# A decoder layer on one core: seven products for eight over both halves of a down product, and work moved off VectorE

## The chip, the cores and the metric

The kernel runs on one core of a Trainium2 chip. The metric is the device time of one execution in microseconds (us). The engines are TensorE (PE, with PEld for its weight loads), VectorE (DVE), ScalarE (ACT), GpSimd (POOL) and SyncE (SP), each with a queue that it works through in order; DMA transfers are issued from the queues of SP and POOL.

## What is computed

One decoder layer over x of 2 x 512 tokens with 1024 features, all in fp32, with three normalisations:

```
x = layernorm(x + attention(x))        # per token: 32x32 scores between features d and e, over 32 heads
x = layernorm(x + crossing(x, ctx))    # fake_quant(x) @ fake_quant(ctx), 8 bits, ctx 1024x1024
x = layernorm(x + ffn(x))              # below
h = relu(x @ up) ** 2                  # up 1024x2048
latent = x @ fc1                       # fc1 1024x512
moe = (latent @ expert) * (sum of the two largest of x @ gate)
ffn = layernorm(h @ down + moe @ fc2, gamma, beta)     # down 2048x1024, fc2 512x1024
```

The attention mixes features within a token: scores are (d, e) for each token, summed over heads, with a softmax over e. It is therefore elementwise work and reductions on VectorE, not matmuls.

## The kernel before

The 1024 tokens are eight tiles of 128 (`NT = 8`), paired in four blocks of 256 tokens (`TB = 2` tiles a block). The product expert·fc2 is made once (`e2`), so that the end of the ffn is one product: the 2048 squares and 512 latents of a token, as `h` of five groups (`NG = 5`) of four slices of 128 (`piece`), times the rows of down and of e2.

In time the kernel goes: a front of 142.5 us (q, k, v of all tiles, e2, attention and crossing of tiles 0 and 1), then block 0 (`ffn`, its up and fc1 products at line 827 until 219 us, and its down product `down`, line 1057, until 296 us), then block 1 (up and fc1 until 376 us, its down product `down_halved` until 450.4 us), then blocks 2 and 3 together (`ffn_pair`, `down_pair`, from 454.7 us) until the end at 697.3 us. While TensorE multiplies for blocks 0 and 1, VectorE does the attention of tiles 2 to 7, whose results the pair needs.

Several generators make this order. `token_path` walks through the tiles: `scores` (lines 474 and 480, a multiplication of 128x2048 and a reduction, four of each a tile), `attend` (lines 507 and 513, the same number), `cross`. `ffn` walks through the matmuls of a block and is paced against the token path by weights (`w_ffn`, `w_tok`). Side work stands in the list `later`, and `beside(n)` steps each entry n times after a product; `tc.issue_after(x)` keeps an instruction behind x in the scheduler's order, and within that the scheduler of the framework sets the queues. `behind_products` keeps transposes and products in the order of the program on TensorE, behind the latest matmul.

`cross` quantises a tile into `a` (a pass on ACT of `below_top` for most tiles, `quantise` on VectorE for the two of the front, which are `hurried`), transposes it (`pta`, line 652) into `aT` by a copy on ACT (line 653), multiplies by the codes of the context (`py`, line 665), and adds that to `xc` (lines 658, 659 and 670). `between` holds the score steps of the next tile, placed in its middle. Then `normalise_aside` normalises with ACT and POOL: sums, squares (line 351), the power on POOL (line 355) and the scaled pass (line 360). The context's tiles are made into codes by `context_beside`, with three tiles loaded ahead.

PSUM has two banks for `product` (`ps_mm`), four for the down products (`ps_dn`) and two for transposes (`ps_tr`). In `ffn` a relu on ACT (line 843) empties a product bank, and a second pass (line 844) squares it into `h`. In `down` (block 0) the columns are done in halves of 512 with plain products of 128x512; at the end `finish` takes each tile straight from PSUM on VectorE: statistics (lines 324 and 326), a scaled difference with gamma (line 1006), and the sum with xc (line 1013, which also sums for the last normalisation), then `store_aside`.

`down_halved` (block 1) makes its left 512 columns with plain products (line 1109): for each group and slice k, one matmul for each of the two tiles. Its right 512 columns go by a scheme of seven products for eight (line 1129). The block is seen as 2 x 2: the two tiles by the two column quarters of 256, with the contraction in pairs of slices. VectorE makes sums of the weights (`sums_of`, lines 1097 to 1100, four of 128x512 a group) and of `h` (lines 1088 to 1091, four of 128x256), and TensorE does seven products of 128x256 for each of two slices:

```
1088  nc.vector.tensor_tensor(s1, a21[:, g], a22[:, g], ALU.subtract)
...
1097  nc.vector.tensor_tensor(t1, b11, b12, ALU.add)
```

The seven products collect over the five groups in four PSUM banks (1 and 6, 7 and 5, 4, 2 and 3), and after the last group VectorE combines them into `c11` to `c22`. The two tiles are then normalised with gamma in `ended_later`.

Of the kernel before, what the change touches and what calls it, by code (L numbers as in the profile page):

```python
# [16 lines left out]
P = 128  # L17
EPS = 1e-5
# [9 lines left out]
def kernel(  # L28
# [288 lines left out]

    def mean_rstd(halves, name, stats=None):
# [9 lines left out]
        nc.vector.tensor_scalar_add(ve, mv[:, 1:2], EPS)  # L328
# [4 lines left out]
    def normalise(t, name):  # L333

        mean, rstd = mean_rstd([t[:, ts(h, HALF)] for h in range(E // HALF)], name)
        return nc.vector.tensor_scalar(t, t, mean, rstd, ALU.subtract, ALU.mult)
# [25 lines left out]
    def quantise(dst, src, tmp, rs, z):  # L362

        nc.vector.tensor_scalar(tmp, src, rs, z, ALU.mult, ALU.add)
        nc.vector.tensor_scalar(tmp, tmp, 0.0, QMAX, ALU.max, ALU.min)
        nc.vector.tensor_scalar(dst, tmp, ROUND, ROUND + CENTRE, ALU.add, ALU.subtract)
# [100 lines left out]
    def scores(t, qk, behind=None):  # L467
# [3 lines left out]
        for c in range(D // DC):  # L471
            prod = tokp.tile([P, DC * D * G], F32, tag="prod", name=f"pqk_{t}_{c}", bufs=2)
            with tc.issue_after(behind.ins) if behind is not None else ExitStack():
                nc.vector.tensor_tensor(  # L474
# [5 lines left out]
            nc.vector.tensor_reduce(  # L480
                s[:, ts(c, DC), :].rearrange("p d e -> p (d e)"),
                prod.rearrange("p (c g) -> p c g", g=G), AX.X, ALU.add,
            )
            yield 4.6
# [12 lines left out]
    def attend(t, xc, s, v):  # L497
# [7 lines left out]
        for c in range(D // DC):  # L505
            prod = tokp.tile([P, DC * D * G], F32, tag="prod", name=f"pav_{t}_{c}", bufs=2)
            nc.vector.tensor_tensor(  # L507
                prod.rearrange("p (d g e) -> p d g e", d=DC, g=G),
                s[:, ts(c, DC), :].unsqueeze(2).to_broadcast([P, DC, G, D]),
                v.unsqueeze(1).to_broadcast([P, DC, G, D]),  # L510
                ALU.mult,
            )
# [9 lines left out]
        if t == TB - 1:  # L522

            nc.vector.tensor_tensor(x3, x3, o3, ALU.add)
            normalise(xc, f"1_{t}")
# [23 lines left out]
    def context_beside(b):  # L549


        stages = {}

        def load(k):
            if k < KC:
                stages[k] = pools["sums"].tile([P, E], F32, tag="tt", name=f"ctx_{b}_{k}")

                nc.gpsimd.dma_start(stages[k], ctx_in[b, ts(k, P), :])

        passes = {}  # L560
        for k in range(3):
            load(k)
        for k in range(3):
# [7 lines left out]
        for k in range(KC):  # L571
# [9 lines left out]
            load(k + 3)  # L581
# [34 lines left out]
    def cross(t, xc, cq, crow, between):  # L616
# [6 lines left out]
        if hurried:  # L623

            quantise(a, xc, tmp, rs1, z1)
# [14 lines left out]
        else:  # L640
# [7 lines left out]
            yield from between  # L648
# [6 lines left out]
        behind = ExitStack if hurried or t == NT - 1 else lambda: tc.issue_after(lowered[0].ins)  # L655
        r = small.tile([P, 1], F32, tag="r", name=f"r_{t}")
        with behind():
            nc.vector.tensor_mul(r, total, s12d2)
# [18 lines left out]
        else:  # L677
            yield 3.0
            last = yield from normalise_aside(xc, sums, f"2_{t}")
            yield 6.0  # L680
        return last

    def token_path():


        batch, last = None, None
        at, done = {}, {}

        def begin(t):
# [5 lines left out]
            at[t] = xc, v, scores(t, qk, last if t == TB else None)  # L695
# [13 lines left out]
        for blk in range(NBLK):  # L709
            xcs = []  # L710
            x2T = []
            for i in range(TB):
# [4 lines left out]
                if t == 0:  # L717

                    begin(1)
                    yield next(at[1][2])  # L720
                yield from attend(t, xc, done[t], v)
# [6 lines left out]
                last = yield from cross(t, xc, *batch, between)  # L728
# [86 lines left out]
    def ffn(blk, xcs, xT):  # L815
# [21 lines left out]
        for c in range(INT // CW):  # L837
# [9 lines left out]
            if c in (1, INT // CW - 2):  # L847
                next(routing)
        for c in range(LAT // CW):
            w = wstream.tile([P, KE, CW], F32, tag="wa", name=f"fc1_{blk}_{c}")  # L850
            nc.sync.dma_start(w, fc13[:, :, ts(c, CW)])
            for i in range(CW // P):
# [12 lines left out]
        yield from (down if blk < PAIR - 1 else down_halved)(blk, h)  # L865
# [180 lines left out]
    def down(blk, h):  # L1046
# [16 lines left out]
        for i in range(TB):  # L1063
            finish(blk, i, new_y(blk, i), pd[i])

    def down_halved(blk, h):

        def rows_of(g, n):
            count[0] += 1
            pool, tag = (pools["more"], "wc") if count[0] % 3 == 0 else (wstream, "wb")  # L1070
            w = pool.tile([P, 4, HALF], F32, tag=tag, name=f"dn_{blk}_{n}_{g}")
            src, at = (dn3, 4 * g) if 4 * g < NI else (e23, 4 * g - NI)
            rows_loaded[0] = nc.sync.dma_start(w, src[:, at : at + 4, ts(n, HALF)])
            return w
# [3 lines left out]
        )  # L1078
        units, weights = {}, {}

        def sums_of(g):
            w = rows_of(g, 1)
# [3 lines left out]
            ss = pools["more"].tile([P, 4, 2, P], F32, tag="ss", name=f"units_{blk}_{g}", bufs=3)  # L1086
            s1, s2, s3, s4 = (ss[:, q] for q in range(4))
            nc.vector.tensor_tensor(s1, a21[:, g], a22[:, g], ALU.subtract)
            nc.vector.tensor_tensor(s2, s1, a11[:, g], ALU.subtract)
            nc.vector.tensor_tensor(s3, a11[:, g], a21[:, g], ALU.subtract)  # L1090
            nc.vector.tensor_tensor(s4, a12[:, g], s2, ALU.add)
            units[g] = {
                1: a11[:, g], 2: a12[:, g], 3: s4, 4: a22[:, g], 5: s1, 6: s2, 7: s3
            }
            tt = pools["sums"].tile([P, 3, 2, QW], F32, tag="tt", name=f"halved_{g}")
# [5 lines left out]
            weights[g] = {1: b11, 2: b21, 3: b22, 4: t4, 5: t1, 6: b12, 7: t3}  # L1101

        pd = [ps_dn.tile([P, HALF], F32, tag="dn", name=f"pd_{blk}_{i}") for i in range(TB)]
        for g in range(NG):
            w = rows_of(g, 0)
            for k in range(4):
                for i in range(TB):
                    with behind_products():
# [462 lines left out]
```

## Time and profile before

| what | value |
|---|---|
| time, median of 3 runs | 699.71 us (699.28 to 700.66) |
| the profiled execution | 699.09 us, span 697.3 us |
| mean granted clock of TensorE in it | 0.993 |
| TensorE busy | 677.7 us, 97% |
| VectorE busy | 607.5 us, 87% |
| ScalarE busy | 263.7 us, 38% |
| GpSimd busy | 76.0 us, 11% |
| block 1, plain left half (line 1109) | 80 records of 128x512, 376.9 to 416.1 us with other work between |
| block 1, seven-product right half (line 1129) | 140 records of 128x256, 416.1 to 450.4 us |

A matmul in fp32 leaves two records, so 80 records are 40 matmuls. The times of the profile are from the start of the span. A line of a timeline names start, length, engine, source line, operation, what it writes and reads, and in brackets the idle time before it and what ended that. In the windows, a row gives start and end, the length, the busy time with the number of instructions of PE, PEld, DVE, ACT and POOL, the granted clock of TensorE as a share, the share of the DMA engines and GB/s. In the list of waits the three numbers are the total, how often, and the longest.

### The profile page before, as it was taken

What the parts mean: (1) busy time and instruction counts of PE and PEld (TensorE: products, weight loads), DVE (VectorE), ACT (ScalarE), POOL (GpSimd) and SP (SyncE); (2) the same over time, 40 slices, a digit from 0 to 9 for tenths busy, and PEclk for the clock granted to TensorE, in tenths of its full rate; (3) what the DMA queues carried; (4) which work ended last, traced back from release to release, by engine and by line L of the source; (5) the groups of instructions that cost most, each with busy time, mean ns of one, the idle gap of its engine ahead of it and who ended that gap; (6) DMA issues with size and microseconds to landing.
All of it is one profiled execution on the core that took longest, in us unless ns stands there. A gap on an engine that the chain in (4) does not pass through costs nothing.

```text
span 697.3 us, 7629 instructions
## 1 busy us (share of the span) xinstructions
PE 677.7 (97%) x2862; PEld 494.6 (71%) x2872; DVE 607.5 (87%) x724; ACT 263.7 (38%) x443; POOL 76.0 (11%) x107
## 2 busy tenths in 40 slices
PE   8999999999999999999999999999999999999991
PEld 4666654578877444478877458788888888888881
DVE  5899987699999999799999987698778679897895
ACT  1287543222635449627726215311144200000252
POOL 1012112200011122002001000020011000000012
PEclk9999999999999999999999999999999999999997
DMA  9999628394545548455535534695887545557733
GB/s 335 302 335 366 156 25 299 102 305 144 166 135 160 193 140 292 136 180 189 176 126 153 163 117 170 210 335 197 305 305 277 193 141 180 178 185 193 213 76 121
DMA packets 73460, 139.08 MB, mean 199 GB/s; under 512 B 5264, under 2 KB 39696, under 8 KB 73424
## 3 DMA queue, kind: packets, MB, share of 16 engines
q1 hardware_dynamic: 63216, 106.87, 45.3%
q0 software_dynamic: 10064, 31.47, 16.1%
q8 instruction: 22, 0.36, 0.2%
q10 hardware_dynamic: 144, 0.26, 0.1%
q14 instruction: 14, 0.11, 0.0%
HBM read 114.99 MB, written 21.50 MB: 196 GB/s over the span
## 4 chain that ended last, share of the span: by engine, by line
PE 46%; DVE 4%; ACT 3%; DMA 2%; issue 1%; POOL 1%; POOLq 0%; DVEq 0%; ACTq 0%
PE pp L942 9%; PE ps L1401 5%; PE pu L827 5%; PE pp_mm L942 5%; PE pd L1109 5%; PE ph L1129 4%; PE pp_tr L942 4%; PE ps_mm L1401 2%; PE pl L827 2%; PE ps_tr L1401 2%; PE py L665 1%; DMA dn<-tw 1%; ACT square L351 1%; DMA y_a<-xc 1%; DVE pav L507 1%
## 5 line engine op out<-in xcount | busy, mean ns | idle before, releaser
L827 PE MATMUL pu<-x2T,up 128*128 128x256 f32 x512 | 113.1, 380 | 0.8 <-ACT relu L843 0.8
L827 PEld LDWEIGHTS pu<-x2T,up 128*128 128x128 f32 x512 | 96.5, 190 | 14.9 <-ACT relu L843 1.2
L474 DVE TENSOR_TENSOR pqk<-qk 128x2048 f32<-128x2048 f32 x32 | 72.5, 2282 | 0.0
L507 DVE TENSOR_TENSOR pav<-s,v 128x2048 f32<-128x2048 f32 x32 | 72.4, 2281 | 0.0
L480 DVE TENSOR_REDUCE s<-pqk 128x256 f32<-128x2048 f32 x32 | 72.3, 2277 | 0.1
L513 DVE TENSOR_REDUCE o<-pav 128x64 f32<-128x2048 f32 x32 | 72.0, 2265 | 0.0
L1057 PE MATMUL pd<-dn,h 128*128 128x512 f32 x160 | 69.5, 593 | 0.0
L157 PE MATMUL pqk<-wqkv,xT 128*128 128x512 f32 x128 | 63.4, 595 | 0.9 <-DVE wqkv L249 0.6
L1057 PEld LDWEIGHTS pd<-dn,h 128*128 128x128 f32 x160 | 30.2, 190 | 36.2 <-issue 35.9
L162 PEld LDWEIGHTS pv<-wqkv,xT 128*128 128x128 f32 x128 | 24.3, 190 | 24.2 <-issue 22.5
L355 POOL TENSOR_TENSOR rstd<-ve,neg_half 128x1 f32<-128x1 f32 x21 | 19.7, 939 | 167.0 <-ACT ve L353 129.3
L162 PE MATMUL pv<-wqkv,xT 128*128 128x256 f32 x128 | 35.6, 379 | 0.0
L1109 PE MATMUL pd<-dn,h 128*128 128x512 f32 x80 | 35.0, 593 | 0.0
L843 ACT ACTIVATE relu<-pu 128x256 f32<-128x256 f32 x32 | 12.1, 377 | 52.1 <-PE pu L827 52.1
L157 PEld LDWEIGHTS pqk<-wqkv,xT 128*128 128x128 f32 x128 | 23.6, 190 | 11.1 <-issue 4.5
L1305 DVE TENSOR_TENSOR tt<-dn 128x1024 f32<-128x1024 f32 (+1 forms) x20 | 21.2, 1058 | 11.2 <-DMA dn<-in_L_ffn_down_w_dram 6.9
L665 PE MATMUL py<-cq,aT 128*128 128x512 bf16 x120 | 27.4, 379 | 1.5 <-ACT aT L653 1.1
L458 PE MATMUL pe<-fc,exT 128*128 128x512 f32 x64 | 28.7, 594 | 0.0
L827 PE MATMUL pl<-x2T,fc 128*128 128x256 f32 x128 | 28.0, 379 | 0.0
L1109 PEld LDWEIGHTS pd<-dn,h 128*128 128x128 f32 x80 | 15.0, 190 | 17.4 <-issue 17.2
L827 PEld LDWEIGHTS pl<-x2T,fc 128*128 128x128 f32 x128 | 24.3, 190 | 3.4
L665 PEld LDWEIGHTS <-aT 128*128 128x128 bf16 x128 | 12.4, 98 | 16.6 <-ACT aT L653 1.5
(338 smaller groups left out, 1274.6 us busy)
## 6 DMA issues: line engine op xcount, KB each, us to landing
up<-in_L_ffn_up_w_dram SPq DMA_DIRECT2D x16, 1024.0 KB, 5.4
dn<-in_L_ffn_down_w_dram SPq DMA_DIRECT2D x16, 1024.0 KB, 5.0
pair<-in_L_ffn_up_w_dram SPq DMA_DIRECT2D x8, 1024.0 KB, 6.7
dn<-tw SPq DMA_DIRECT2D x8, 1024.0 KB, 5.0
tw<-outer POOLq DMA_DIRECT2D x7, 1024.0 KB, 5.5
fc<-in_L_ffn_fc_w_dram SPq DMA_DIRECT2D x6, 1024.0 KB, 5.7
dn<-in_L_ffn_down_w_dram SPq DMA_DIRECT2D x12, 512.0 KB, 5.4
outer<-in_L_ffn_down_w_dram SPq DMA_DIRECT2D x5, 1024.0 KB, 5.4
```

The source lines that it names most:

```text
L157: projecting[0] = nc.tensor.matmul(pqk, xT[:, k, :], wqkv[k][:, 0 : 2 * DG], start=(k == 0), stop=(k == KE - 1))
L162: nc.tensor.matmul(pv[:, :DG], xT[:, k, :], wqkv[k][:, 2 * DG : 3 * DG], start=(k == 0), stop=(k == KE - 1),)
L474: nc.vector.tensor_tensor(prod.rearrange("p (d e g) -> p d e g", d=DC, g=G), q3[:, ts(c, DC), :].unsqueeze(2).to_broadcast([P, DC, D, G]), ...
L480: nc.vector.tensor_reduce(s[:, ts(c, DC), :].rearrange("p d e -> p (d e)"), prod.rearrange("p (c g) -> p c g", g=G), AX.X, ALU.add,)
L507: nc.vector.tensor_tensor(prod.rearrange("p (d g e) -> p d g e", d=DC, g=G), s[:, ts(c, DC), :].unsqueeze(2).to_broadcast([P, DC, G, D]), ...
L513: nc.vector.tensor_reduce(o[:, ts(c, DC), :].rearrange("p d g -> p (d g)"), prod.rearrange("p (c e) -> p c e", e=D), AX.X, ALU.add,)
L665: crossed[t] = nc.tensor.matmul(py, aT[:, k, :], cq[:, k, ts(h, HALF)], start=(k == 0), stop=(k == KC - 1))
L827: lately[0] = nc.tensor.matmul(ps[:, :NB], ws[:, k, wcols], xT[:, k, :], start=(k == 0), stop=(k == KE - 1))
L942: lately[0] = nc.tensor.matmul(banks[m], steps[g][m][:, k, :], moving[m][:, k, :], start=(k == 0 and m not in (6, 3, 7)), stop=(k == KH - ...
L1057: lately[0] = nc.tensor.matmul(pd[i][n], h[:, kk // 4, i, kk % 4, :], w[:, k, ts(n, HALF)], start=(kk == 0), stop=(kk == NK - 1),)
L1109: lately[0] = nc.tensor.matmul(pd[i], h[:, g, i, k, :], w[:, k, :], start=(g == 0 and k == 0), stop=(g == NG - 1 and k == 3),)
L1401: lately[0] = nc.tensor.matmul(banks[mm], unit(o, mm, j), inner_weights[o, cc][mm][:, j - lo, :], start=(j == 0 and mm not in FIRST_OF), s ...
```

## The change

1. Both halves of the columns of block 1 go by seven products for eight. The sums of `h` that both halves need (`s1`, `s2`, and `s3`, written over a21) are made once; `s4` and the weights' sums for each half and group. The first two groups are prepared during the last fc1 product. Two of the weight tiles use the buffers `wa` of the up product. The combinations are done twice, and their order is changed.
2. Tile 2's scores begin earlier: one multiplication in the wait for rstd of tile 1, and a reduction and a multiplication in tile 1's wait in its crossing (`early_step`). `w_tok` starts at 6.9 to match.
3. The finish of block 0 leaves VectorE: ACT copies PSUM and sums, `normalise_aside` follows, VectorE multiplies by gamma, an accumulating DMA issued by POOL adds xc, ACT sums, and `store_aside` ends it as before.
4. `context_beside` loads five tiles ahead in place of three.
5. In the crossing of tile 6 only one score step of the next tile stands in its middle, and the rest come after it; the additions of tile 6 (lines 658 and 659) are, as those of tile 7 were before, no longer kept behind the pass of the next tile's scores at line 490 (`lowered`), and one multiplication of tile 7's attention is kept behind tile 6's addition.

```
+    def normalise(t, name, meanwhile=False):
 
         mean, rstd = mean_rstd([t[:, ts(h, HALF)] for h in range(E // HALF)], name)
-        return nc.vector.tensor_scalar(t, t, mean, rstd, ALU.subtract, ALU.mult)
+        with early_step(measured[0]) if meanwhile else ExitStack():
+            return nc.vector.tensor_scalar(t, t, mean, rstd, ALU.subtract, ALU.mult)
+
+    early, turn, stepped = [None], [None], [None]
+
+    def early_step(behind, n=1):
+
+        turn[0] = behind
+        for _ in range(n):
+            next(early[0])
+        return tc.issue_after(stepped[0].ins)
...
+            with tc.issue_after(turn[0].ins) if t == TB else ExitStack():
+                stepped[0] = nc.vector.tensor_tensor(
                     prod.rearrange("p (d e g) -> p d e g", d=DC, g=G),
                     q3[:, ts(c, DC), :].unsqueeze(2).to_broadcast([P, DC, D, G]),
                     k3.unsqueeze(1).to_broadcast([P, DC, D, G]),
                     ALU.mult,
                 )
-            nc.vector.tensor_reduce(
-                s[:, ts(c, DC), :].rearrange("p d e -> p (d e)"),
-                prod.rearrange("p (c g) -> p c g", g=G), AX.X, ALU.add,
-            )
-            yield 4.6
+            if t == TB:
+                yield 2.3
+            with tc.issue_after(turn[0].ins) if t == TB else ExitStack():
+                stepped[0] = nc.vector.tensor_reduce(
+                    s[:, ts(c, DC), :].rearrange("p d e -> p (d e)"),
+                    prod.rearrange("p (c g) -> p c g", g=G), AX.X, ALU.add,
+                )
+            yield 2.3 if t == TB else 4.6
...
+            crossing = (t, c) == (NT - 1, 2)
+            with tc.issue_after(tokens_added[0].ins) if crossing else ExitStack():
...
-            normalise(xc, f"1_{t}")
+            normalise(xc, f"1_{t}", True)
...
+        extra = pools["more"].tile([P, 2, NG, 2, P], F32, tag="ss", name=f"ctx_{b}")
+        extra = extra.rearrange("p s j k n -> p (s j k n)")
 
         def load(k):
             if k < KC:
-                stages[k] = pools["sums"].tile([P, E], F32, tag="tt", name=f"ctx_{b}_{k}")
+                if k in (3, 4):
+                    stages[k] = extra[:, ts(k - 3, E)]
+                else:
+                    stages[k] = pools["sums"].tile([P, E], F32, tag="tt", name=f"ctx_{b}_{k}")
 
                 nc.gpsimd.dma_start(stages[k], ctx_in[b, ts(k, P), :])
 
         passes = {}
-        for k in range(3):
+        for k in range(5):
...
-            quantise(a, xc, tmp, rs1, z1)
+            rounded = quantise(a, xc, tmp, rs1, z1)
+            waited = early_step(rounded, 2)
...
-            yield from between
+            if t == NT - 2:
+                between = iter(between)
+                yield next(between)
+            else:
+                yield from between
...
-        behind = ExitStack if hurried or t == NT - 1 else lambda: tc.issue_after(lowered[0].ins)
+        behind = ExitStack if hurried or t >= NT - 2 else lambda: tc.issue_after(lowered[0].ins)
         r = small.tile([P, 1], F32, tag="r", name=f"r_{t}")
+        with waited if hurried else behind():
+            nc.vector.tensor_mul(r, total, s12d2)
         with behind():
...
+            if t == NT - 2:
+                yield from between
...
+                if t == TB - 1:
+                    begin(TB)
+                    early[0] = at[TB][2]
...
-                last = yield from cross(t, xc, *batch, between)
+                turn[0] = yield from cross(t, xc, *batch, between)
...
+        halved = blk == PAIR - 1
+        rows = (down_halved if halved else down)(blk, h)
         for c in range(LAT // CW):
             w = wstream.tile([P, KE, CW], F32, tag="wa", name=f"fc1_{blk}_{c}")
             nc.sync.dma_start(w, fc13[:, :, ts(c, CW)])
+            if halved and c == LAT // CW - 1:
+                next(rows)
...
-        yield from (down if blk < PAIR - 1 else down_halved)(blk, h)
+        yield from rows
...
-            finish(blk, i, new_y(blk, i), pd[i])
+            y = new_y(blk, i)
+            sums = small.tile([P, 2], F32, tag="sum2_y", name=f"sum2_y_{blk}_{i}")
+            for n in range(2):
+                acted[0] = nc.scalar.activation(
+                    y[:, ts(n, HALF)], pd[i][n], AF.Copy, accum_out=sums[:, n : n + 1]
+                )
+            later.append(finish_aside(blk, i, y, sums))
+
+    def finish_aside(blk, i, y, sums):
+
+        yield
+        yield from normalise_aside(y, sums, f"f_{blk}_{i}")
+        yield
+        nc.vector.tensor_tensor(y, y, gamma, ALU.mult)
+        nc.gpsimd.dma_start(y, xcs_of[blk][i], accum_op=ALU.add)
+        for _ in range(8):
+            yield
+        sums = small.tile([P, 1], F32, tag="sum3", name=f"sum3_{blk}_{i}")
+        square = attp.tile([P, E], BF16, tag="square", name=f"summed_{blk}_{i}")
+        acted[0] = nc.scalar.activation(square, y, AF.Copy, accum_out=sums)
+        yield from store_aside(of[ts(blk * TB + i, P), :], y, sums, f"3_{blk}_{i}", 0)
...
     def down_halved(blk, h):
...
+        ss = pools["more"].tile([P, 2, NG, 2, P], F32, tag="ss", name=f"units_{blk}")
+        s1, s2 = ss[:, 0], ss[:, 1]
+        units, weights = {}, {}
+        def sums_of(n, g):
+            c = NG * n + g
+            pool, tag = (
+                (pools["more"], "wc") if c in (2, 7) else (wstream, "wa" if c in (3, 4) else "wb")
+            )
             w = pool.tile([P, 4, HALF], F32, tag=tag, name=f"dn_{blk}_{n}_{g}")
             src, at = (dn3, 4 * g) if 4 * g < NI else (e23, 4 * g - NI)
             rows_loaded[0] = nc.sync.dma_start(w, src[:, at : at + 4, ts(n, HALF)])
...
+            if n == 0:
+                nc.vector.tensor_tensor(s1[:, g], a21[:, g], a22[:, g], ALU.subtract)
+                nc.vector.tensor_tensor(s2[:, g], s1[:, g], a11[:, g], ALU.subtract)
+                nc.vector.tensor_tensor(a21[:, g], a11[:, g], a21[:, g], ALU.subtract)
+            s4 = pools["more"].tile([P, 2, P], F32, tag="s4", name=f"s4_{n}_{g}", bufs=3)
+            nc.vector.tensor_tensor(s4, a12[:, g], s2[:, g], ALU.add)
...
-        pd = [ps_dn.tile([P, HALF], F32, tag="dn", name=f"pd_{blk}_{i}") for i in range(TB)]
-        for g in range(NG):
-            w = rows_of(g, 0)
-            for k in range(4):
-                for i in range(TB):
-                    with behind_products():
-                        lately[0] = nc.tensor.matmul(
-                            pd[i], h[:, g, i, k, :], w[:, k, :],
-                            start=(g == 0 and k == 0), stop=(g == NG - 1 and k == 3),
-                        )
-                if k % 2 == 1:
-                    beside(2)
-                    yield 3.5
-                if (g, k) == (NG - 1, 1):
-                    sums_of(0)
-        sums_of(1)
+            weights[n, g] = {1: b11, 2: b21, 3: b22, 4: t4, 5: t1, 6: b12, 7: t3}
+
+        order = [(n, g) for n in range(2) for g in range(NG)]
+        for at in order[:2]:
+            sums_of(*at)
+        yield
         ys = [new_y(blk, i) for i in range(TB)]
-        for i in range(TB):
-            acted[0] = nc.scalar.copy(ys[i][:, 0:HALF], pd[i])
-        b = [ps_dn.tile([P, 2, QW], F32, tag="dn", name=f"ph_{blk}_{i}") for i in range(4)]
-        banks = {1: b[0][:, 0], 6: b[0][:, 1], 7: b[1][:, 0], 5: b[1][:, 1],
-                 4: b[2][:, 0], 2: b[3][:, 0], 3: b[3][:, 1]}
-        for g in range(NG):
+        for at, (n, g) in enumerate(order):
+            if g == 0:
+                b = [
+                    ps_dn.tile([P, 2, QW], F32, tag="dn", name=f"ph_{blk}_{n}_{i}")
+                    for i in range(4)
+                ]
+                banks = {1: b[0][:, 0], 6: b[0][:, 1], 7: b[1][:, 0], 5: b[1][:, 1],
+                         4: b[2][:, 0], 2: b[3][:, 0], 3: b[3][:, 1]}
             for mm in (1, 6, 7, 5, 4, 2, 3):
...
                 if mm == 5:
-                    if g + 2 < NG:
-                        sums_of(g + 2)
+                    if at + 2 < len(order):
+                        sums_of(*order[at + 2])
                     beside(2)
-                    yield 4.0
+                    yield 3.5
             beside(2)
-            yield 4.0
-        (c11, c12), (c21, c22) = (
-            [y[:, HALF + e * QW : HALF + (e + 1) * QW] for e in range(2)] for y in ys
-        )
-        acted[0] = nc.scalar.copy(c11, banks[1])
-        nc.vector.tensor_tensor(c12, banks[6], c11, ALU.add)
-        nc.vector.tensor_tensor(c22, banks[7], c12, ALU.add)
-        nc.vector.tensor_tensor(c21, banks[4], c22, ALU.add)
-        for c in (c12, c22):
-            nc.vector.tensor_tensor(c, banks[5], c, ALU.subtract)
-        nc.vector.tensor_tensor(ys[0][:, HALF:], b[3].rearrange("p a b -> p (a b)"), ys[0][:, HALF:], ALU.add)
+            yield 3.5
+            if g < NG - 1:
+                continue
+            (c11, c12), (c21, c22) = (
+                [y[:, n * HALF + e * QW : n * HALF + (e + 1) * QW] for e in range(2)] for y in ys
+            )
+            acted[0] = nc.scalar.copy(c11, banks[1])
+            nc.vector.tensor_tensor(c12, banks[6], c11, ALU.add)
+            nc.vector.tensor_tensor(c22, banks[7], c12, ALU.add)
+            nc.vector.tensor_tensor(c12, banks[5], c12, ALU.subtract)
+            nc.vector.tensor_tensor(c21, banks[4], c22, ALU.add)
+            nc.vector.tensor_tensor(c22, banks[5], c22, ALU.subtract)
+            y = ys[0][:, ts(n, HALF)]
+            nc.vector.tensor_tensor(y, b[3].rearrange("p a b -> p (a b)"), y, ALU.add)
...
-    w_tok, w_ffn, alive = 0.0, 0.0, True
+    w_tok, w_ffn, alive = 6.9, 0.0, True
```

## The prediction

> **What bounds the kernel now.** I read the table of engines first, then the slices, then the waits of TensorE, and then the chain of waits and the windows around the second block.
>
> ```profile
> PE 677.7 (97%) x2862; PEld 494.6 (71%) x2872; DVE 607.5 (87%) x724; ACT 263.7 (38%) x443; POOL 76.0 (11%) x107
> PE   8999999999999999999999999999999999999991
> PEclk9999999999999999999999999999999999999997
> ```
>
> TensorE (PE) is busy for 677.7 of 697.3 us at full clock, so time goes where its work goes, and a gain can come only from fewer or faster matmuls or from its few gaps:
>
> ```profile
> PE py L665 <- ACT aT L653: 1.1, 1, 1.1
> PE pu L827 <- ACT relu L843: 0.8, 1, 0.8
> 199.08 3.40 PE L665 MATMUL py<-cq,aT 128*128 128x512 bf16 x15 [1.08 <-ACT aT L653]
> 323.41 27.89 PE L827 MATMUL pu<-x2T,up 128*128 128x256 f32 x128 [0.81 <-ACT relu L843]
> ```
>
> These two are the only gaps over 0.6 us after the start. The second block's down product as the chain has it (start, length, records):
>
> ```profile
> 379.66 29.19 PE pd L1109 x68
> ...
> 416.24 21.58 PE ph L1129 x100
> ```
>
> The plain left half runs at 29.19 / 68 = 0.4293 us a record, the seven-product right half at 21.58 / 100 = 0.2158. Windows of the stage before it, of its left half and of its right half (PE, PEld, DVE, ACT, POOL):
>
> ```profile
> 297.00:376.00 79.00, 78.08 (x380) 65.35 (x375) 79.00 (x80) 36.43 (x78) 5.92 (x10) 1.00 0.50 162
> 376.00:416.00 40.00, 39.95 (x120) 18.86 (x120) 39.72 (x38) 12.19 (x19) 2.38 (x3) 1.00 0.54 158
> 416.08:450.41 34.33, 34.28 (x166) 28.69 (x166) 22.03 (x43) 15.99 (x29) 1.66 (x3) 1.00 0.49 174
> ```
>
> VectorE (DVE) has no free time from 297 to 416, and 34.33 - 22.03 = 12.3 us behind that. So in this stretch PE sets the time and DVE is full beside it: work added to DVE before 416 arrives late by its whole length.
>
> **The change, part by part.**
>
> *Matmuls.* Line 1109's 80 records of 128x512 go (80 x 0.4293 = 34.34 us), and 5 groups x 7 products x 2 x 2 records = 140 of 128x256 come (140 x 0.2158 = 30.21). That is -4.13. Weight loads do not bind at this shape: in the right half PEld is busy 28.69 of 34.33 while PE has no gap.
> The Trainium skill ("TensorE: Matmul & The Clock Gate", section "Back-to-back issue gap") speaks against narrow matmuls: each carries a fixed 2.5 ns over N/2.4 ns, and weight loads share the spacing. As an estimate from that page, two passes a record, the two sides would be 34.5 and 30.6, a gain of 4.0; the rows here decide.
>
> *The gap at 199.08* (1.08). The exponent pass that ACT ran ahead of aT moves earlier, with tile 2's scores begun early. -1.08; bounds -1.08 and 0.
>
> *The gap at 323.41* (0.81). It is a relu behind 5.9 us of other ACT work. The order of that work changes wholly, so I count -0.81 here and what replaces it below.
>
> *DVE, front.* Tile 2's first score steps (2.20 us each) go into two waits of DVE:
>
> ```profile
> 119.54 0.81 DVE L336 TENSOR_SCALAR xc<-xc,mv,rstd 128x1024 f32<-128x1024 f32 x1 [3.08 <-POOL rstd L330]
> 127.04 0.16 DVE L658 TENSOR_TENSOR r<-pr,s12d 128x1 f32<-128x1 f32 x1 [4.38 <-PE pr L636]
> ```
>
> One step fits in 3.08, two (4.40) in 4.38. DVE gains 6.6 us; the two waiting lines slip by at most 0.1. PE has other products there, so nothing on the path by itself.
>
> *DVE, first block's end.* The finish leaves DVE (4 statistics of 0.6, 4 adds of 0.67, 2 of 1.2, small ones: 7.9 us). Back come two multiplies by gamma, 2 x 1.14 = 2.3. ACT takes 4 PSUM copies of 0.56, two normalisations of about 3.4 (square 1.15+0.19, y 1.23, four small ones) and two sums of 1.06: 11 us more in the 79 us stage that has 36.43. POOL issues two accumulating transfers y<-xc, 4.5 us to landing each by the like one y_a<-xc.
>
> *DVE, second block.* Added: 4 weight sums of 0.60 for each of 5 groups (12.0), one s4 of 0.335 a group (1.7), and a second set of combinations (5 x 0.335 + 0.60 = 2.3). Net against the stages before: 12.0 + 1.7 + 2.3 + 2.3 - 7.9 - 6.6 = +3.8 us, less than the 12.3 us that DVE has free behind 416. In total it fits. The question is when.
>
> *New wait at the PSUM banks.* The first half takes all four banks of the down pool, and the second half takes the same four, in the same order; before, the right half found two banks free. So the second half's products 7 and 5 wait until DVE has done with bank 1, in the last but one of its combinations, and DVE is in order: ahead of it stand the scheduled sums and tile 7's attention.
> PE: 376.0 + 1.74 (transposes) + 30.21 + 0.45 + 3.40 (tile 6's pta and py) = 411.8, and 1.73 later (products 1 and 6) it needs bank 1, at 413.5. DVE: tile 7's attention now ends at 411.74 + 0.08 (line 528). In the new queue the release stands behind all this but the last 5.9 us of it, with these in addition: 25 weight sums of 0.60 (15.0), ten of `h` (3.35), the combinations (2.3), gamma (2.3) and tile 6's two additions (1.3), less 7.9 and 6.6 and the 1.1 us that DVE waits at 155 for an exponent. 411.7 - 5.9 + 24.3 - 15.6 = 414.5; with waits of its own up to 416.4. So PE waits 1.0 to 2.9; I take +1.6. Bounds: 0 (DVE early, as in the right half's rows) and +4 (a weight load late as in line 1097's 1.6 us idle on a DMA, on top).
> The Trainium skill ("Perfetto Trace Analysis", section on matmuls) says that independent groups of matmuls should rotate through different banks of PSUM so that emptying one overlaps the next group, which this change gives up. By that rule alone the wait would be the whole chain of the seven combinations, 0.4 + 5 x 0.335 + 0.60 = 2.7 us; no run here shows it yet.
>
> *New waits on ACT.* (a) At 264.32 PE transposes tile 3's xc, which ACT finished at 264.17. PE now comes about 2 us earlier (262.3 by its queue: 1.08 of it is the gap at 199.08, the rest small gaps of the front), ACT's 1.23 us pass is done at 262.5 to 263.6 because DVE's front work is earlier too: +0.7, bounds 0.25 and 1.5. (b) ACT is in order, and relu, which empties one of two product banks, stands behind the two `summed` passes, which wait for the accumulating transfers. PE can run 3.5 us (a product) before it feels it: +0.9, bounds 0 and 2.4. (c) The same with the first block's stores, whose ACT passes of 1.15 and 1.23 come in front of a later relu: +0.4, bounds 0 and 1.2; the row for the price is 323.41, 5.9 us of ACT for 0.81 of PE.
>
> *The rest.* Five context tiles loaded ahead for three, the split of the last crossings and tile 7's pinned product move work that hides under the matmuls: 0, unless DVE's lateness reaches tile 7's a, whose transpose on PE stands at 437.66 and has about 2 us of margin. The two weight tiles that go to the other buffers put the pair's first loads behind the last down loads on SP; the pair starts 4.27 us after the down product (450.41 to 454.71), a load is 5.0 to 6.7 us and has tens of us: 0.
>
> From 454.71 on PE has no gap (122.00 of 122.00 in 455 to 577), so what is won before comes out at the end.
>
> **Sum**, against the profiled execution (699.09, of which 697.3 is span): -4.13 - 1.08 - 0.81 + 1.6 + 0.7 + 0.9 + 0.4 = -2.4, so 696.7. The median of the three runs (699.71) is 0.6 above it: 697.3. With every unknown at its good end 693.7, at its bad end 702.8.
>
> **Rivals.** 0.2% (1.4 us) is about what a measurement here can tell from no change: faster is below 698.3, slower above 701.1.
>
> *A. No new waits of note* (693.7 to 695.5): DVE comes earlier than my walk, and two product banks cover ACT. For it: ACT is at 46% in that stage, and DVE's total fits. Against: DVE's 100% rows. 0.14.
>
> *B. DVE too late at the bank* (slower). Each us that DVE's last release of the first half's bank 1 lies behind PE's 413.5 costs PE a us, since no other product is ready. Without that wait the sum is -4.0, so the change is a loss beyond 5.4 us, that is when the release comes after 418.9; 702 at 6.3 us. For it: 38 DVE operations without a gap in 376 to 416, and 12.0 us of sums put just there. Against: my walk ends 2.5 us short of it. 0.18.
>
> *C. ACT holds PE in the second block's first product* (698.5 to 700.5): (a), (b) and (c) at their upper ends (5.1 for 2.0) leave -2.4 + 3.1 = +0.7, 700.4; half of that, 698.9. For it: the relu of 323.41. 0.15.
>
> *D. It does not do what it says*: the narrow matmuls of a whole stage run at PEld's pace, or starved of sums, and the 4.13 do not come: 701.4. The right half's row speaks against it. 0.03.
>
> **How the numbers follow.** My own case (695.5 to 699.5) has 0.50, of it 0.38 below 698.3. Faster: 0.38 + 0.14 + 0.02 of C = 0.54. Slower: B, D and none of C = 0.20 (a little of B ends within the bound). Same: 0.26. The range 695.0 to 701.3 leaves out about 0.08 of A and 0.13 of B. My case alone is 695.5 to 699.5.
>
> **What would show it.** Right: 280 ph records at 0.216 each and no pd record in the second block; line 665's wait at 199 gone; a gap of PE at the first ph of the second half, ended by DVE's combination; DVE's waits of 3.08 and 4.38 filled; small gaps of pu behind relu and of pt_x behind tile 3's xc. Wrong: a first-half time over 30.5 without transposes and py (starved of sums); gaps of relu over 2.5 in all; pta of tile 7 waiting for DVE; any new gap behind 455, above all at the first pair loads; or a clock below 0.99.

## The result and the profile after

The changed kernel takes 706.75 us (median of four runs, 705.71 to 709.89) against 699.73 before: a ratio of 1.0106, with an interval of 1.0073 to 1.0139. It is 7.0 us slower; I had forecast 697.3 and a range up to 701.3. The profiled execution took 706.85 us with a span of 705.1.

TensorE is busy for as long as before (677.1 us for 677.7), and the line of its clock is the same but for the last slice. The loss shows in the slices of TensorE, where one reads 7 and one 8 around the middle (slices of 17.6 us; the 7 covers 317 to 335 us). From the page of the changed kernel, the line of the engines and the slices of TensorE:

```profile
PE 677.1 (96%) x2932; PEld 506.2 (72%) x2932; DVE 617.8 (88%) x741; ACT 273.3 (39%) x468; POOL 81.6 (12%) x109
PE   8999999999999999997989999999999999999991
```

The waits of TensorE name what stands there (in total, how often, the longest, in us):

```profile
PE pu L862 <- ACT relu L878: 7.5, 3, 3.4
...
PE pt_x L134 <- ACT xc L372: 1.2, 1, 1.2
PE ph L1179 <- DVE y L1197: 1.1, 1, 1.1
```

The gap at 199 us is gone. In its place stand three gaps in front of `pu` in block 1's up product. The timeline of TensorE, and windows behind the longest gap (the eighth field, after the five engines, is the granted clock):

```profile
320.90 3.72 PE L862 MATMUL pu<-x2T,up 128*128 128x256 f32 x16 [1.16 <-ACT relu L878]
328.05 26.13 PE L862 MATMUL pu<-x2T,up 128*128 128x256 f32 x112 [3.44 <-ACT relu L878]
357.03 3.72 PE L862 MATMUL pu<-x2T,up 128*128 128x256 f32 x16 [2.85 <-ACT relu L878]
```

```profile
326.00:328.00 2.00, 0.00 (x0) 0.00 (x0) 2.00 (x4) 1.42 (x4) 0.00 (x0) 1.00 0.85 301
328.00:330.00 2.00, 1.95 (x6) 1.68 (x7) 2.00 (x5) 1.97 (x6) 0.00 (x0) 0.70 0.96 327
330.00:332.00 2.00, 2.00 (x6) 1.55 (x6) 0.59 (x1) 0.60 (x2) 0.96 (x1) 0.50 1.09 370
332.00:334.00 2.00, 2.00 (x11) 1.71 (x10) 0.00 (x0) 0.47 (x2) 0.00 (x0) 0.95 0.12 38
```

After the gap of 3.44 us TensorE runs at half clock for about 4 us: six records in 2 us for eleven. The 112 records of that row take 26.13 us; at the 0.2179 us a record of the row of before (27.89 for 128) they would take 24.4. So the gap costs another 1.7 us.

Why relu is late stands in the queue of ACT, which works in order (timeline of ACT):

```profile
319.00 0.30 ACT L371 ACTIVATE shift<-rstd,minus 128x1 f32<-128x1 f32 x1 [2.97 <-POOL rstd L367]
...
320.48 0.36 ACT L878 ACTIVATE relu<-pu 128x256 f32<-128x256 f32 x1
323.12 1.06 ACT L1122 ACTIVATE summed<-y 128x1024 bf16<-128x1024 f32 x1 [2.28 <-DMA y<-xc]
...
326.58 1.06 ACT L1122 ACTIVATE summed<-y 128x1024 bf16<-128x1024 f32 x1 [2.00 <-DMA y<-xc]
...
327.64 0.36 ACT L878 ACTIVATE relu<-pu 128x256 f32<-128x256 f32 x1
...
354.98 0.29 ACT L371 ACTIVATE shift<-rstd,parts 128x1 f32<-128x1 f32 x1 [2.39 <-POOL rstd L367]
```

In front of the first two gaps ACT mostly waits, and relu stands behind what it waits for: 2.97 us for a power on POOL, and 2.28 and 2.00 for the accumulating transfers. In front of the third, 7.5 us pass between two relus (349.12 to 356.62): 2.6 of them are waits for powers, and the rest is ACT's own work for the stores. The transfers took 7.6 and 9.7 us to landing (4.5 for the like transfer before), and some powers are long (timeline of POOL):

```profile
308.32 2.67 POOL L367 TENSOR_TENSOR rstd_f<-ve_f,neg_half 128x1 f32<-128x1 f32 x1 [9.37 <-ACT ve_f L365]
311.66 0.54 POOL L367 TENSOR_TENSOR rstd_f<-ve_f,neg_half 128x1 f32<-128x1 f32 x1 [0.66 <-ACT ve_f L365]
...
316.76 3.08 POOL L1117 DMA_DIRECT2D y<-xc  x1
...
351.61 3.34 POOL L367 TENSOR_TENSOR rstd<-ve,neg_half 128x1 f32<-128x1 f32 x1 [0.66 <-ACT ve L365]
```

The same one-column power takes 0.54 us or, in the three longest rows of this stage, 2.67, 2.80 (at 316.18) and 3.34. The slow ones lie over VectorE's 128x2048 multiplications (308.28 to 310.57, 316.29 to 318.58, 351.66 to 353.94, the last with an addition of 128x512 behind it to 354.54), and each ends 0.4 us after these; the fast one at 311.66 lies beside short additions and the reduction. The Trainium skill ("SBUF — State Buffer", section "Who interferes with whom") says that a VectorE instruction with two inputs in SBUF contends with a GpSimd instruction that reads SBUF, and that whichever issues first blocks the other for its whole length. The rows agree that the two exclude each other; but in two of the three the power's row begins 0.05 and 0.11 us before the multiplication's, and it is still the power that waits. The issue of 3.08 us stands behind the power of 2.80 in POOL's queue and ends 0.86 us after it, so it is no sign that VectorE holds up an issue; the other issue took 0.93.

Why the transfers landed late is not shown. The DMA engines were full (share 0.98 to 1.09) from 318 to 326 us, but in run 2 below, with a share of 1.02 and more from 318 to 324, the two took 4.8 and 7.4 us.

Where the 7.8 us of span went: TensorE comes to block 1's down product at 386.02 instead of 376.04, 9.98 later (7.45 - 0.81 of relu, 1.7 of clock, 0.6 brought along from before the stage, and 1.0 left over, which is no idle time: beside the three gaps TensorE is idle for 0.14 us from 297 to 386), and the down product then takes 71.96 us (to 457.98) for 74.21 (to 450.25). From the pair's first product (462.4 for 454.6) to the end both kernels are alike.

### The profile page after: what moved, and what is told of

It is laid out like the page before. It is cut to its first block, busy times and chain, and to the rows that moved or that the text cites. A ratio compares the mean times of both kernels' runs of the same rounds, so it can differ in the third digit from the quotient of the medians.

```text
span 705.1 us, 7819 instructions
## 1 busy us (share of the span) xinstructions
PE 677.1 (96%) x2932; PEld 506.2 (72%) x2932; DVE 617.8 (88%) x741; ACT 273.3 (39%) x468; POOL 81.6 (12%) x109
## 4 chain that ended last, share of the span: by engine, by line
PE 67%; DVE 14%; ACT 9%; issue 5%; DMA 2%; POOL 2%; SPq 0%; POOLq 0%; DVEq 0%; ACTq 0%
PE pu L862 11%; PE pp L981 9%; PE pqk L157 8%; PE ps L1454 7%; PE pp_mm L981 5%; PE ph L1179 4%; PE pv L162 4%; PE pp_tr L981 4%; PE ps_mm L1454 4%; PE pe L472 3%; PE ps_tr L1454 3%; DVE pav L526 3%; DVE o L532 3%; PE py L695 2%; DVE s L497 2%
## 5 line engine op out<-in xcount | busy, mean ns | idle before, releaser
L862 PE MATMUL pu<-x2T,up 128*128 128x256 f32 x512 | 115.5, 385 | 7.5 <-ACT relu L878 7.5
L1096 PE MATMUL pd<-dn,h 128*128 128x512 f32 x160 | 69.5, 593 | 0.0
L1096 PEld LDWEIGHTS pd<-dn,h 128*128 128x128 f32 x160 | 30.2, 190 | 36.2 <-issue 35.9
L367 POOL TENSOR_TENSOR rstd<-ve,neg_half 128x1 f32<-128x1 f32 x21 | 21.9, 1041 | 172.5 <-ACT ve L365 169.2
L695 PE MATMUL py<-cq,aT 128*128 128x512 bf16 x128 | 28.9, 379 | 0.0
L1179 PE MATMUL ph<-dn,h 128*128 128x256 f32 x80 | 20.7, 381 | 1.1 <-DVE y L1197 1.1
L358 ACT ACTIVATE parts<-sum 128x1 f32<-128x1 f32 (+1 forms) x21 | 4.0, 197 | 44.6 <-DVE xc L700 20.9
```

Source lines behind the costliest of these rows:

```text
L695: crossed[t] = nc.tensor.matmul(py, aT[:, k, :], cq[:, k, ts(h, HALF)], start=(k == 0), stop=(k == KC - 1))
L862: lately[0] = nc.tensor.matmul(ps[:, :NB], ws[:, k, wcols], xT[:, k, :], start=(k == 0), stop=(k == KE - 1))
L1096: lately[0] = nc.tensor.matmul(pd[i][n], h[:, kk // 4, i, kk % 4, :], w[:, k, ts(n, HALF)], start=(kk == 0), stop=(kk == NK - 1),)
```

## The experiments

Two theories. The first: the cost is the moved finish of block 0, and of it the waits of ACT in front of relu. The rival: the load of VectorE (before, it is at 100% from 297 to 416 us, and the change adds to it). The table gives all runs, each against runs of the kernel before on the same chip (medians of 699.2 to 699.7).

| run | us | ratio (interval) |
|---|---|---|
| changed kernel | 706.75 | 1.0106 (1.0073 to 1.0139) |
| 1 finish back on VectorE | 699.89 | 1.0003 (0.9987 to 1.0019) |
| 2 the moved finish alone | 707.78 | 1.0108 (1.0079 to 1.0137) |
| 3 the seven products alone | 707.67 | 1.0113 (1.0088 to 1.0137) |
| 4 addition on VectorE | 704.07 | 1.0062 (1.0042 to 1.0081) |
| 5 sums on ACT later | 702.49 | 1.0028 (1.0006 to 1.0050) |
| 6 early combinations | 703.54 | 1.0042 (1.0021 to 1.0063) |
| 7 statistics on ACT | 703.35 | 1.0046 (1.0026 to 1.0066) |
| 8 three context tiles | 707.86 | 1.0102 (1.0077 to 1.0126) |
| 9 the front's part alone | 698.62 | 0.9985 (0.9971 to 1.0000) |
| 10 tile 7's transposes later | 705.11 | 1.0080 (1.0055 to 1.0104) |
| 11 front, and tile 3 first | 702.22 | 1.0039 (1.0025 to 1.0053) |

**1. Undo the moved finish.**

```diff
-            y = new_y(blk, i)
...
-            later.append(finish_aside(blk, i, y, sums))
+            finish(blk, i, new_y(blk, i), pd[i])
```

> The changed kernel with the first block's finish back on VectorE (part 3 undone, all else kept). Theory (ACT's queue holds relu behind the moved finish: gaps of 1.16, 3.44 and 2.85 us on TensorE, and about 2 us of half clock behind the longest): relu gaps fall to under 1.5 us in all, the clock stays at 1.00 after the first block, 9.4 us come back; VectorE has 5.6 us more, so the wait at the PSUM bank grows from 1.3 to 3 to 7: 699 to 703. Rival (VectorE's load is the cause, its work delays everything): the time rises, above 707. Rival (the context tiles or the order of the front): the gaps stay, 706.

All relu gaps are gone, and 6.9 us come back of the 9.4 expected; the bank takes 2.1 us (1.9 and 0.2), less than the 3 to 7 expected. But the kernel is only as fast as before. Of the 4.13 us that the narrow matmuls save, 3.9 are spent on waits behind VectorE, 2.1 at the banks and 1.8 at tile 7's transposes, whose `a` ACT starts on as soon as VectorE lets it. The third line is mostly (1.1) the gap before tile 3's transposes (waits of TensorE, and ACT's row):

```profile
PE ph L1159 <- DVE y L1177: 1.9, 1, 1.9
PE pta L681 <- ACT a L669: 1.8, 1, 1.8
PE pt_x L134 <- ACT xc L372: 1.4, 2, 1.1
```

```profile
435.18 0.20 ACT L358 ACTIVATE parts<-sum 128x1 f32<-128x1 f32 x1 [27.75 <-DVE xc L547]
```

VectorE ends tile 7's attention at 435.07 us, 23 us later than before (411.74). In the changed kernel it ends at 435.16, just as late, but TensorE, some 10 us late itself, does not wait for it at tile 7. Both theories hold, then, each for its own part: the finish on ACT makes the loss, and VectorE takes the gain.

**2. The moved finish alone, in the kernel before.** The edit is the reverse of the last, on the kernel before.

> The kernel before with part 3 alone (the first block's finish on ACT, gamma on VectorE, the sum by an accumulating transfer). Theory: the same kind of relu gaps, 4 to 8 us, and a clock drop where one is over 3 us: 702 to 709. Rival (the finish on ACT only hurts because the seven products' sums make VectorE late with gamma): gaps under 2 us, 699 to 701.

The loss is there without the seven products (+8.2 us): gaps of 1.9 and 3.6 behind relu, 1.4 for a load of `up`, and the clock at 0.54 and 0.60 in the 4 us after the longest (waits of TensorE):

```profile
PE pu L827 <- ACT relu L843: 5.5, 2, 3.6
PE pu L827 <- DMA up<-in_L_ffn_up_w_dram: 1.4, 1, 1.4
```

The rival, that the products' sums make it late, falls. But here ACT's work counts too: in front of the gap of 3.6, 10.1 us pass between two relus (340.11 to 350.17), of which 2.1 are waits for powers; the rest is mostly three normalisations that come together.

**3. The seven products alone, in the kernel before.**

> The kernel before with part 1 alone (both halves by seven products, no relief of VectorE). Theory: no new relu gaps; 4.1 us of matmuls go; VectorE, 16 us fuller and with none of its 14.5 us of relief, releases the banks of the first half and tile 7's a late: 4 to 12 us of waits on it in the block's down product: 700 to 708. Rival (VectorE's idle time behind 416 absorbs it): 695.5 to 697.

As expected, +8.1 us: without relief VectorE is too late, and it shows at tile 7 (waits of TensorE):

```profile
PE pt_x L134 <- ACT xc L360: 4.1, 1, 4.1
PE pta L652 <- ACT a L644: 2.7, 1, 2.7
```

Both gaps are followed by half clock. Between the two halves, where I had looked for the wait at the bank, there is none; the pair's first product waits 0.5 us for a combination. One relu gap is 1.3 us (0.8 before).

**4 and 5. What ACT waits for.** Run 4 puts the addition on VectorE and drops the transfer and ACT's sum; run 5 keeps all work and only puts the sums later:

```diff
-        nc.gpsimd.dma_start(y, xcs_of[blk][i], accum_op=ALU.add)
...
-        acted[0] = nc.scalar.activation(square, y, AF.Copy, accum_out=sums)
+        nc.vector.scalar_tensor_tensor(y, y, 1.0, xcs_of[blk][i], ALU.mult, ALU.add, accum_out=sums)
```

```diff
-        for _ in range(8):
+        for _ in range(14):
             yield
         sums = small.tile([P, 1], F32, tag="sum3", name=f"sum3_{blk}_{i}")
```

> The changed kernel with the accumulating transfer and ACT's summing pass replaced by one addition with a sum on VectorE for each tile (2 x 1.2 us). Theory: ACT no longer waits for a transfer in front of relu: the gap of 3.44 us and the clock drop behind it (5.4 us) go, the two others (4.0 us) stay or move: 699.5 to 703.5. Rival (it is ACT's load, not its wait for the transfer): gaps of 6 us and more stay, 705 to 707.

> The changed kernel with ACT's two summing passes six steps of the side work later, so that the accumulating transfers have landed when ACT comes to them; nothing is taken away. Theory (ACT waits for the transfers in front of relu): the gap of 3.44 us and the half clock behind it go (5.4 us), the gaps by the POOL powers (1.16 and 2.85) stay or move: 700 to 703. Rival (it is the sheer load of ACT): gaps of 6 us and more, 705 to 708.

Run 5 leaves ACT's load as it was (busy 273.7 us for 273.3) and brings the relu gaps from 7.45 to 1.4 us, 4.3 us of time (waits of TensorE):

```profile
PE pu L862 <- DMA up<-in_L_ffn_up_w_dram: 2.2, 1, 2.2
PE pu L862 <- ACT relu L878: 1.4, 2, 1.2
```

So the order in ACT's queue decides, and not ACT's total load. The 4.3 us are not the price of the transfers alone: the gap of 2.85 went as well, since the stores' powers now come at 359.82 and 361.32 and take 0.54 and 1.03 us. It is no clean win: a load of `up` comes 2.2 us late, and half clock follows again. Runs 2 and 5 have such a late load and run 1 has none; whether the accumulating transfers hold the loads up was not tested. In run 4 the transfer's gap is gone (0.9 and 2.25 are left), but the time, just above my range, keeps the gap of 2.25 with its half clock and 2.0 in front of tile 7's transposes.

**6 to 8, 10. Can the rest be won?** Run 6 is run 1 with the combinations of banks 0 and 1 issued before the last three products, and the second half's groups from last to first, so that three `s4` are used twice; run 7 is run 6 with statistics of block 0 by ACT; run 8 is run 7 with three context tiles; run 10 is run 7 with tile 7's transposes later.

```diff
+                    if last:
+                        acted[0] = nc.scalar.copy(c11, banks[1])
+                        nc.vector.tensor_tensor(c12, banks[6], c11, ALU.add)
+                        nc.vector.tensor_tensor(c21, banks[7], c12, ALU.add)
+                        nc.vector.tensor_tensor(c12, banks[5], c12, ALU.subtract)
+                        nc.vector.tensor_tensor(c22, banks[5], c21, ALU.subtract)
```

```diff
+            nc.scalar.activation(junk[:, ts(n, HALF)], parts[n], AF.Copy, scale=1.0 / E, accum_out=both[:, n : n + 1])
...
+            acted[0] = nc.scalar.activation(junk[:, ts(n, HALF)], parts[n], AF.Square, scale=1.0 / 32.0, accum_out=both[:, 2 + n : 3 + n])
```

```diff
-            yield 2.0
+            yield 12.0 if t == NT - 1 else 2.0
```

> The finish on VectorE again, and in the block's down product the combinations of banks 0 and 1 are issued before the last three products of a half, with c22 made straight from bank 5 (the same number of operations), and the second half takes the groups from last to first, so that three of the s4 sums are used twice (1.0 us less on VectorE). Theory (VectorE's whole load up to tile 7's attention sets the end, the bank is only where it shows): what is won at the bank comes back at tile 7's transpose, and only the 1.0 us stays: 698.5 to 699.5. Rival (the bank wait is a cost of its own): 2.1 us and more come off, below 698.

> As the run with the early combinations, and the first block's statistics come from ACT (a sum and a sum of squares of each PSUM half, 8 passes of 0.6 us, in the 10 us in which ACT is idle at the end of the first block's down product); the rest of the finish stays on VectorE, which has 2.6 us less. Theory (VectorE sets the end, and ACT work there hurts only when it waits in front of relu): another 2 to 2.6 us come off, 696 to 697.5, with no relu gap over 0.5. Rival (any added ACT work delays relu): gaps of relu over 1 us, 699 or more.

> As the run with the statistics on ACT, with three context tiles ahead as before the change (part 4 undone). Theory: the gap of 1.1 us before tile 3's transposes (264 us) goes, and, if VectorE is no longer the bound there, the time falls by up to 1.1: 695 to 697. Rival (the gap is off the path, since VectorE is late anyway): the same time as with five tiles, within 0.4.

> As the run with the statistics on ACT, with tile 7's transposes of a put about four products later on TensorE, nothing added or taken away. Theory (the 3.6 us gap in front of these transposes, and the half clock behind it, come from the place in TensorE's queue; the chain behind VectorE's last attention step still sets when tile 7 is done): the gap falls under 1.5 us, the clock stays, part of it comes back before tile 7's last transposes: 699 to 701.5. Rival (VectorE's lateness costs the same wherever TensorE waits): within 0.7 of the 703.4 of that run.

All four missed. In run 6 bank 0 no longer waited, but the scheduler put a reduction of tile 7's attention (128x2048, 411.64 to 413.83) between the combinations; the one for bank 1 ended at 415.5, and the wait came back there as a gap of 2.40 us. That trace is of the shortest of twelve executions (700.87 us); what the others lost beside it, up to the median of 703.54, no trace shows. Run 7 did bring VectorE to the end of tile 7's attention at 431.14, 3.9 us sooner than run 1, but TensorE came sooner too, and the gap before tile 7's transposes grew (timeline and windows of run 7):

```profile
440.58 1.04 PE L681 MATMUL pta<-identb,a 128*128 128x128 bf16 x8 [3.64 <-ACT a L669]
```

```profile
440.50:442.00 1.50, 1.42 (x10) 1.33 (x11) 1.44 (x3) 0.37 (x2) 0.00 (x0) 0.50 0.00 0
442.00:444.00 2.00, 2.00 (x6) 1.44 (x5) 1.72 (x3) 0.67 (x1) 0.00 (x0) 0.50 0.00 0
```

Run 7 also has a relu gap of 1.7 us, as its rival had it.

Run 10 takes that gap away and in its trace keeps the clock at 1.00 there, and is no faster (705.11 for 703.35): waits come back as 1.1 us behind VectorE's addition in the crossing and 1.6 behind ACT's normalising pass (451 and 457 us), and 2.4 for a load of the pair (496 us). Run 8 shows the other end of the same: with three tiles the gap at 264 us is still 0.7, tile 7's transposes wait 3.4 us, and a load of the pair is 5.3 us late (`pp` behind DMA, at 509 us). What stays open is which change of the order makes the pair's loads late in runs 8 and 10.

**9 and 11. The front's part by itself.** Run 9 is the kernel before with part 2; run 11 also keeps the context's passes behind tile 3's normalising pass.

> The kernel before with part 2 alone: tile 2's first score steps in VectorE's two waits of the front, nothing else. Theory (the relief by itself is sound; the gap of 1.08 us at 199 us goes, and VectorE's lead changes nothing on TensorE elsewhere): 698.0 to 699.2, with VectorE 6 us earlier at tile 7's attention (406 for 411.7). Rival (the lead moves other waits in front of TensorE, as at tile 3's transposes): 699.6 or more.

> The run with part 2 alone, and the second half's context passes on ACT are kept behind tile 3's normalising pass, so that TensorE's transposes of tile 3 (a gap of 1.1 us at 264 us) find it done. Theory (that gap is on the path, TensorE being the bound before the pair): 1.1 us comes off, 697.2 to 698.0. Rival (the context's codes come late instead, and TensorE waits for them at about 285 us or at tile 4's product): 698.5 or more, with a gap there.

Run 9 is the only one with a median below that of before, by 0.7 us or 0.15%, within the range forecast for it; its interval ends at 1.0000, so that it is not clear of no change. VectorE ends tile 7's attention at 405.89 us, as expected. The gap at 199 us goes (1.08), and 1.1 us comes in front of tile 3's transposes, as the trace of the longest of its twelve executions (701.44 us) has it. Run 11, meant to take that away, missed: it has 1.3 us there all the same (TensorE comes to these transposes at 259.5 rather than 263.8), and a relu gap of 2.4 us with half clock behind it (timelines of TensorE and ACT, run 11):

```profile
324.91 29.58 PE L854 MATMUL pu<-x2T,up 128*128 128x256 f32 x128 [2.38 <-ACT relu L870]
```

```profile
319.58 0.29 ACT L372 ACTIVATE shift<-rstd,parts 128x1 f32<-128x1 f32 x1 [5.30 <-POOL rstd L368]
```

Here the finish is still on VectorE, and the same kind of wait holds relu up: ACT stood 5.30 us in front of a store's power, and that power stood in POOL's queue behind an issue that waited for VectorE until 316.9.

## Why the prediction was wrong

- *Matmuls, -4.13.* Right in size: in the new first half 48 records take 10.36 us (389.50 to 399.86), 0.2158 each, without a gap for sums.
- *The gap at 199, -1.08.* Right; it is gone in every run with part 2 but for 0.25 us.
- *The bank, +1.6.* Right in size (1.12 and 0.20; run 1 has 1.9 and 0.2), with two differences. The longer wait is at the first of the four banks, and not at bank 1. And in the changed kernel both sides are later than in the forecast: TensorE needs the first bank at about 422.1, and the combination that frees it ends at 423.2, where the forecast had 413.5 and 414.5 to 416.4 for bank 1. That the difference comes out although both are late is partly luck.
- *Tile 3's transposes, +0.7 (0.25 to 1.5).* Right: 1.16.
- *Relu behind `summed` (b), +0.9 with an upper end of 2.4, and behind the stores (c), +0.4 with 1.2.* This is the step that failed. Measured: 1.16 (behind the power of 2.80 us) + 3.44 + 1.7 of clock, and 2.85, together 9.2 us for 1.3, and above both upper ends; the prediction's own sign of error, relu gaps over 2.5 us in all, came with 7.45. I priced (c) by the row at 323.41, a train of ACT's *work* (5.9 us for 0.81), and (b) by no row but the 3.5 us that a product covers. What ACT meets in front of the first two gaps are *waits* for two other queues. The transfer's length was taken from one row, 4.5 us (7.6 and 9.7 here), and the powers were given none (2.80 and 3.34 here), though the trace before held one of 2.44 us (at 207.38). For (c) the row itself was too kind: in run 2 three normalisations that come together, with 2.1 us of waits, hold relu up until TensorE stands for 3.6 us. Rival C named the place, but it was bounded by the same upper ends.
- *The clock.* I named it only as a sign of error. It was a term: the gap of 3.44 us brought a second loss of 1.7 us.
- *The rest, 0.* These terms together make -4.13 - 1.08 - 0.81 + 1.3 + 1.2 + 9.2 = +5.7 of the 7.8 us measured. The other 2 us are spread over the stages in pieces of 0.5 to 1.0, for which the sum had no term, and which no run here explains.
- *The bounds.* The measured 706.75 lies above the bad end of all unknowns too, 702.8 (703.9, if the gap at 199 is also put at its own bound of 0, which that figure leaves at -1.08; the good end is 693.9 by the stated bounds; the pair starts 4.30 us after the down product, not 4.27). So no choice within the bounds gives the result: the terms of relu and the clock lay outside them.
- *VectorE's balance.* The net +3.8 us fits into 12.3 us of idle time only if that time lies before the work that waits. It lies behind it. Tile 7's `a`, for which I had put 0 with about 2 us of margin, costs 1.8 us in run 1, and with the 2.1 at the banks nearly the whole gain of the matmuls goes there.

## What to carry to other kernels

Before work is moved to an engine that is mostly idle, look at what the moved instructions wait for and at what stands behind them in that engine's queue: here two waits of 2.3 and 2.0 us in front of the instruction that empties a product bank stood before a gap of 3.44 us of TensorE. When matmuls are cut by an algorithm that adds vector work, count the vector engine's idle time only where it lies ahead of its next consumer. And a gap on TensorE is not always worth its length alone: behind some gaps of 2.2 us and more the clock cost another 1.7 us here.

## What the runs showed of the hardware

- Gaps of TensorE and the clock behind them: full clock after 1.16, 1.80, 1.86, 1.90, 2.00, 2.39, 2.40, 2.85 and 3.43 us; half clock after 2.20, 2.25, 2.38, 2.66, 3.44, 3.60, 3.64, 4.12 and 5.26. So no fixed length between 2.2 and 3.4 us divides the two. The Trainium skill ("TensorE: Matmul & The Clock Gate", on the activity window) speaks of a free-running window of about 3.4 us and of gaps over about 3 us; a window that runs freely would make the outcome depend on where the gap falls, but the drops at 2.20 to 2.66 lie below that figure.
- The price of half clock did not follow the gap's length. After 2.20, 2.25, 2.38, 3.44 and 3.60 us (runs 5, 4, 11, the changed kernel, run 2) it was 1.7 us each time: in run 4, 16 records took 5.41 us for 3.72, in run 2, 32 took 8.86 for 7.15. After 2.66, 3.64, 4.12 and 5.26 us (runs 3, 7, 3 and 8) the clock had fallen before TensorE began again (0.66 to 0.77 over the 2 us before that), and in run 8 it cost more: 16 records took 6.52 us for 3.72.
- The clock may also be why some kernels here scatter: in run 6, three of the four executions at 700.9 to 701.6 us have a mean clock of 0.991 to 0.992 (the fourth 0.989), and those at 703.3 and above 0.988 to 0.990. That is argued from these rows, not shown.
- A one-column power on POOL takes 0.54 us in the shortest rows and up to 3.34 over VectorE's instructions with two inputs in SBUF: in the changed kernel the three longest rows of block 1's up product each end 0.4 us after these.
